# Second graph: own-neighbour mark by a VectorE maximum, shift diagonals by ScalarE instead of GpSimd

## The chip, the cores and the metric

One core of one Trainium2 chip runs the whole program, once per launch. The metric is the device time of that core in microseconds (us); less is better. A core has five engines that each work through their own queue of instructions in order: PE (TensorE, matrix products), DVE (VectorE, element-wise), ACT (ScalarE, functions of one input), POOL (GpSimd, element-wise) and SP (SyncE, which here issues most of the DMAs). They wait for each other by semaphores. "Before" and "after" mean the kernel without and with the change.

## The reference

3327 nodes with 256 features pass through two layers; each is a graph step and a feed-forward step, and each adds to the features `x`. The change lies in the graph step of the second layer, a graph attention:

```python
Wh = x @ W
e_src = Wh @ a[:d_out]
e_dst = Wh @ a[d_out:]
e = leaky_relu(e_src[:, None] + e_dst[None, :], 0.2)
mask = (adj > 0) | jnp.eye(N, dtype=bool)     # every node is its own neighbour
e = jnp.where(mask, e, NEG_INF)
alpha = softmax(e, axis=1)
h = alpha @ Wh
```

`adj` holds zeros and ones, and its diagonal is already one; the kernel pads it with zero rows and columns to 26 tiles of 128 (3328).

## The kernel before

The program runs the first graph, the mixture of experts, the second graph (`graph1`) and the attention heads one after the other. Helpers record every instruction, so that all carry one line (L61), and the profile is read by tile names. The `InOrder` helper of `graph1` keeps every engine's instructions in the order in which the Python code emits them.

`graph1` first joins, normalizes and projects the features (tiles `wh`, `dst`) and then goes through 7 blocks of target nodes (`blocks`: six of 4 tiles, the last of 2). Each block has 26 steps, one for every tile j of source nodes; `steps` is the list of all 182 pairs (b, j), and k counts them. In the loop at line 747, step k emits, in this order: the fixed loads of the next stage (from block 3 on, `heads_fixed`); a row load for the maximum (`load`); where j of step k+2 is a multiple of 4, the next `panel`; then `weights(k+2)`, `sign`, `masked(k+1)`, `gather(k)`, `finish`, `top`; and, at j = 16, 18 and 21, `shifts`, `rows` and `spread_rows` for the next block.

- `panel(b, g)` (line 669): SP loads four source tiles of the adjacency for each of the block's target tiles, one DMA of 256 KB per target tile, into one of three buffers `pan`. The group g = b holds the block's own diagonal squares (128x128). There each square is multiplied by `noti` (ones without the diagonal) and has the identity added, so that its diagonal is one: two POOL instructions for each target tile, 26 tiles in all, lines 677 and 678. Only `masked` of that panel, up to five steps later, needs the result.
- `weights(k)` (681): DVE forms `u` from the two broadcast rows `bc`, ACT takes the exponential.
- `masked(k)` (692): DVE forms `p` from the panel and `u`. `gather(k)` (703): PE multiplies `p` with `wh` into the accumulators `acc` (each product is two matmul records, eight records a step). `u` and `p` have four buffers each.
- `top` (515): in the first 16 steps of a block, DVE reduces eight rows of 1664 signs (tile `sg`) for the next block's maxima; `finish` (713) writes `x` in steps 1 to 4.
- `shifts(b)` (622): from these maxima DVE makes eight columns `ab` of shifts; `dg` is the identity scaled by each of them, two instructions of 128x512. DVE makes them for block 0, POOL for the others (line 639). `rows` multiplies `dg` by ones on PE, `spread_rows` copies the result into `bc` by ACT.
- POOL also makes `noti` once (line 419), issues the DMAs that store `x` (`xs`), and prepares tiles of the next stage (`igw`, `mask`).

Of the kernel before, what the change touches and what calls it, by code (L numbers as in the profile page):

```python
# [12 lines left out]
F32 = mybir.dt.float32  # L13
# [5 lines left out]
ALU = mybir.AluOpType  # L19
# [3 lines left out]
P = 128  # L23
# [78 lines left out]
class Net:  # L102
# [299 lines left out]
    def graph1_weights(self, pool):  # L402

        a = self.a

        self.gw = pool.tile([P, 2, D + 2], F32, name="gw")
        self.nc.scalar.dma_start(
            out=self.gw[:, :, :D], in_=a["gw"].rearrange("(k p) o -> p k o", p=P)
        )
        ga = pool.tile([P, 2 * D], F32, name="ga")  # L410
        self.nc.scalar.dma_start(out=ga, in_=a["ga"].partition_broadcast(P))
        self.vd = pool.tile([P, 2, P], F32, name="vd")
        self.shift = pool.tile([P, 1], F32, name="shift")
        self.noti = pool.tile([P, P], F32, name="noti")
        junk = pool.tile([P, D], F32, name="pj")

        def make(nc, ps):
            gw, shift = self.gw, self.shift
            nc.gpsimd.tensor_tensor(self.noti, self.ones, self.ident, ALU.subtract)
            for k in range(2):  # L420
                for i in range(2):
                    nc.vector.scalar_tensor_tensor(
                        junk, gw[:, k, :D], 1.0, ga[:, ts(i, D)], ALU.mult, ALU.mult,
                        accum_out=gw[:, k, D + i : D + i + 1],
                    )


            sq = junk[:, :2]
            nc.vector.tensor_tensor(sq, gw[:, :, D + 1], gw[:, :, D + 1], ALU.mult)
            nc.vector.tensor_copy(  # L430
                self.vd, gw[:, :, D + 1 : D + 2].to_broadcast([P, 2, P])
            )
            yield 1
            pv = ps()
            for k in range(2):
                nc.tensor.matmul(
                    pv[:, 0, :1], self.ones, sq[:, k : k + 1], start=(k == 0), stop=(k == 1)
                )
            nc.vector.tensor_scalar(shift, pv[:, 0, :1], 1e-30, None, ALU.max)
            nc.gpsimd.tensor_tensor(shift, shift, self.nhalf[:, :1], ALU.pow)  # L440
            nc.vector.reciprocal(shift, shift)
            nc.vector.tensor_scalar(shift, shift, 16.1, 1.0, ALU.mult, ALU.add)

        return make
# [37 lines left out]
    def graph1(self, xs, made, pool):  # L482
        tc, a, x = self.tc, self.a, self.x
        nc = InOrder(tc)
# [4 lines left out]
        with ExitStack() as ctx:  # L489
# [3 lines left out]
            ps = first.enter_context(tc.tile_pool(name="g1ps", bufs=2, space=PSUM))  # L493
            wk = first.enter_context(tc.tile_pool(name="g1w", bufs=4))
            s = self.small
            gw, shift, noti = self.gw, self.shift, self.noti

            W = D + 3
            wh = one.tile([P, NT, W], F32, name="wh")
# [122 lines left out]
            def shifts(b):  # L622


                tiles = blocks[b]
                n, t0 = len(tiles), tiles[0]
                es = e_src[:, t0 : t0 + n]
                m = s.tile([P, 4], F32, tag="m", name="m")[:, :n]
                ab = s.tile([P, 2, 4], F32, tag="ab", name="ab")[:, :, :n]
                for i, t in enumerate(tiles):  # L630
                    nc.vector.tensor_reduce(m[:, i : i + 1], tops.pop(t), AX.X, ALU.max)
                nc.vector.tensor_tensor(m, m, own[:, t0 : t0 + n], ALU.max)
                nc.vector.scalar_tensor_tensor(m, m, shift, es, ALU.subtract, ALU.add)
                nc.vector.scalar_tensor_tensor(m, m, 0.2, m, ALU.mult, ALU.max)
                nc.vector.tensor_tensor(ab[:, 0, :], es, m, ALU.subtract)
                nc.vector.scalar_tensor_tensor(ab[:, 1, :], es, 0.2, m, ALU.mult, ALU.subtract)
                dg = abp.tile([P, 2, 4, P], F32, tag="dg", name="dg1")
                for i in range(2):
                    (nc.gpsimd if b else nc.vector).tensor_tensor(
                        dg[:, i, :n, :],  # L640
                        self.ident.unsqueeze(1).to_broadcast([P, n, P]),
                        ab[:, i, :].unsqueeze(2).to_broadcast([P, n, P]),
                        ALU.mult,
                    )
                return dg

            def rows(b, dg):
# [21 lines left out]
            def panel(b, g):  # L669
                js = min(4, NT - 4 * g)  # L670
                pan = panp.tile([P, 4, 4, P], F32, tag="pan", name="pan1")
                for i, t in enumerate(blocks[b]):
                    nc.sync.dma_start(out=pan[:, i, :js, :], in_=a["adjt"][t][:, ds(4 * g, js), :])
                    if t // 4 == g:

                        d = pan[:, i, t % 4, :]
                        nc.gpsimd.tensor_tensor(d, d, noti, ALU.mult)
                        nc.gpsimd.tensor_tensor(d, d, self.ident, ALU.add)
                pans[b, g] = pan

            def weights(k):
# [49 lines left out]
            nc.vector.tensor_scalar(d2, e_dst, 0.2, None, ALU.mult)  # L731
            nc.vector.tensor_scalar(own, e_dst, shift, None, ALU.add)
            panel(*groups.pop(0))
            panel(*groups.pop(0))
            for k in range(8):
                if k in when:
                    load(*when[k])
            for t in blocks[0]:
                top(t, 2, PARTS[0])
            spread_rows(0, rows(0, shifts(0)))  # L740
            for k in range(3):
                if k in when:
# [4 lines left out]
            for k, (b, j) in enumerate(steps):  # L747

                if b > 2:
                    next(fixed, None)  # L750
                if k + 8 in when:
                    load(*when[k + 8])
                if k + 2 < len(steps):
                    if steps[k + 2][1] % 4 == 0 and groups:
                        panel(*groups.pop(0))
                    weights(k + 2)
                if k + 3 in when:
                    sign(*when[k + 3])
                if k + 1 < len(steps):
                    masked(k + 1)  # L760
                gather(k)
                if b and 1 <= j <= len(blocks[b - 1]):
                    finish(blocks[b - 1][j - 1])
                if k in when:
                    top(*when[k], PARTS[1])
                if b + 1 < len(blocks):
                    if j == 16:
                        dg = shifts(b + 1)
                    if j == 18:
                        pb = rows(b + 1, dg)  # L770
                    if j == 21:
                        spread_rows(b + 1, pb)
# [1244 lines left out]
```

## Time and profile before

| | |
|---|---|
| median of 5 runs | 2944.41 us (2933.12 to 2946.44) |
| the profiled execution | 2942.55 us, its span 2940.9 us |
| DVE, PE, ACT, POOL busy in the span | 2397.9, 2652.6, 1810.4, 972.1 us |
| second graph, blocks 0 to 6 | about 624 to 976 us of the span |
| POOL on `pan` (52 instructions of 128x128) | 447 to 2107 ns each, the two kinds' medians 898 and 782 ns |
| POOL on `dg` (12 instructions) | 1055 to 1489 ns each |

All times inside the profile count from the start of the span. A view by groups gives the count, the busy time and the mean of one shape; a view in order of time gives the start and the length of each instruction, and in square brackets how long its engine was idle before it and who ended that. Consecutive instructions of one engine overlap a little, so the distance from start to start is some hundredths of a microsecond below the length.

### The profile page before, as it was taken

What the parts mean: (1) busy time and instruction counts of PE and PEld (TensorE: products, weight loads), DVE (VectorE), ACT (ScalarE), POOL (GpSimd) and SP (SyncE); (2) the same over time, 40 slices, a digit from 0 to 9 for tenths busy, and PEclk for the clock granted to TensorE, in tenths of its full rate; (3) what the DMA queues carried; (4) which work ended last, traced back from release to release, by engine and by line L of the source; (5) the groups of instructions that cost most, each with busy time, mean ns of one, the idle gap of its engine ahead of it and who ended that gap; (6) DMA issues with size and microseconds to landing.
All of it is one profiled execution on the core that took longest, in us unless ns stands there. A gap on an engine that the chain in (4) does not pass through costs nothing. (4 is left out here: it accounts for less than half of the span.)

```text
span 2940.9 us, 125324 instructions
## 1 busy us (share of the span) xinstructions
PE 2652.6 (90%) x53422; PEld 1961.8 (67%) x53422; DVE 2397.9 (82%) x5619; ACT 1810.4 (62%) x5128; POOL 972.1 (33%) x1448
## 2 busy tenths in 40 slices
PE   7999998878989798999999999999989999999995
PEld 6878887757767666666666666666666666666664
DVE  5102643589999587889989999999999999999997
ACT  6420135555554477778777777777767677676674
POOL 6441634532141146544433333222122222122121
PEclk9999989989999799999999999999999999999998
DMA  9994568647775232333333433333433333433332
GB/s 376 358 324 141 182 208 268 211 177 265 270 245 178 74 91 75 109 100 114 116 102 110 121 116 111 112 116 111 123 113 110 116 115 115 119 114 109 116 110 78
DMA packets 258188, 449.70 MB, mean 153 GB/s; under 512 B 58816, under 2 KB 156608, under 8 KB 257504
## 3 DMA queue, kind: packets, MB, share of 16 engines
q1 hardware_dynamic: 245536, 417.50, 45.0%
q0 software_dynamic: 6576, 18.02, 1.7%
q8 instruction: 421, 6.90, 1.0%
q10 hardware_dynamic: 5520, 6.18, 0.7%
q14 instruction: 135, 1.11, 0.1%
HBM read 393.37 MB, written 25.88 MB: 143 GB/s over the span
## 5 line engine op out<-in xcount | busy, mean ns | idle before, releaser
L61 ACT ACTIVATE sc<-sc,anmax 128x512 f32<-128x512 f32 (+3 forms) x1568 | 1039.8, 668 | 109.0 <-DVE anmax L61 108.7
L61 PEld LDWEIGHTS po<-sc,vr 32*64 32x64 f32 x43728 | 660.8, 131 | 391.2 <-DVE sc L61 235.6
L61 PE MATMUL po<-sc,vr 32*64 32x128 f32 x43728 | 762.8, 275 | 114.0 <-DVE sc L61 75.1
L61 DVE STREAM_TRANSPOSE sc<-sc 128x2048 f32<-128x2048 f32 (+3 forms) x392 | 816.4, 2083 | 26.7 <-ACT sc L61 25.9
L61 PE MATMUL pqk<-kt,qt 64*128 64x512 f32 (+1 forms) x2944 | 738.8, 583 | 20.2 <-ACT qt L61 6.8
L61 DVE TENSOR_SCALAR_CACHE_REDUCE sc<-pqk 128x512 f32<-128x512 f32 (+2 forms) x1152 | 654.9, 623 | 49.8 <-PE pqk L61 48.4
L61 PEld LDWEIGHTS pqk<-kt,qt 64*128 64x128 f32 x2944 | 299.2, 186 | 232.2 <-issue 101.8
L61 PE MATMUL acc<-wh,p 128*128 128x259 f32 x1352 | 310.0, 387 | 34.8 <-DVE p L61 34.8
L61 PEld LDWEIGHTS acc<-wh,p 128*128 128x128 f32 x1352 | 254.1, 191 | 93.0 <-DVE p L61 52.5
L61 PE MATMUL acc<-y,pan 128*128 128x256 f32 x1352 | 304.1, 385 | 11.6 <-DMA pan<-in_adjt_dram 9.9
L61 ACT ACTIVATION_READ_ACCUMULATOR sc<-sc,anmax 128x1 f32 x1568 | 298.7, 191 | 0.0
L61 POOL TENSOR_TENSOR ot<-ot,sxd 128x512 f32<-128x512 f32 x83 | 105.7, 1274 | 579.1 <-ACT ot L61 566.1
L61 PEld LDWEIGHTS acc<-y,pan 128*128 128x128 f32 x1352 | 258.2, 193 | 52.6 <-issue 17.1
L61 DVE CUSTOM_DVE_ANT_0 sc<-pqk,mask 128x512 f32<-128x512 f32 (+3 forms) x416 | 242.3, 636 | 25.0 <-PE pqk L61 24.4
L61 ACT ACTIVATE u<-u,d 128x512 f32<-128x512 f32 (+1 forms) x182 | 125.2, 688 | 159.6 <-DVE u L61 159.3
L61 DVE SCALAR_TENSOR_TENSOR u<-bc,d 128x512 f32<-128x512 f32 (+1 forms) x182 | 136.0, 748 | 0.1
L61 DVE SCALAR_TENSOR_TENSOR p<-pan,u 128x512 f32<-128x512 f32 (+1 forms) x182 | 126.8, 696 | 10.3 <-PE acc L61 6.1
L61 ACT ACTIVATE junk<-ar 128x1664 bf16<-128x1664 f32 x52 | 82.7, 1591 | 65.8 <-DMA ar<-in_adj_dram 64.7
L61 ACT COPY qkv<-ptO 128x256 f32<-128x256 f32 x104 | 38.3, 368 | 134.7 <-PE ptO L61 134.4
L61 PE MATMUL ptO<-igw,ot 128*128 128x68 f32 x832 | 116.7, 283 | 3.7 <-issue 2.0
L61 PEld LDWEIGHTS ptO<-igw,ot 128*128 128x128 f32 x832 | 101.7, 192 | 22.5 <-issue 16.8
L61 DVE CUSTOM_DVE_ANT_0 sg<-sg,dst 128x1664 bf16<-128x1664 bf16 (+2 forms) x56 | 99.9, 1791 | 1.2 <-ACT dst L61 1.0
(340 smaller groups left out, 3020.7 us busy)
## 6 DMA issues: line engine op xcount, KB each, us to landing
vr<-vs SPq DMA_DIRECT2D x976, 128.0 KB
ar<-in_adj_dram SPq DMA_DIRECT2D x104, 832.0 KB
vr<-vs SPq DMA_DIRECT2D x544, 96.0 KB
pan<-in_adjt_dram SPq DMA_DIRECT2D x156, 256.0 KB
pan<-in_adjt_dram SPq DMA_DIRECT2D x26, 1024.0 KB
pan<-in_adjt_dram SPq DMA_DIRECT2D x20, 832.0 KB
w1e<-w SPq DMA_DIRECT2D x59, 256.0 KB
took<-places SPq DMA_DIRECT2D x59, 129.0 KB
```

The lines of the kernel that those rows point to most:

```text
L61: made = make(*args, **kw)
```

## The change

Three edits, all for `graph1`:

```diff
-        self.noti = pool.tile([P, P], F32, name="noti")
...
-            nc.gpsimd.tensor_tensor(self.noti, self.ones, self.ident, ALU.subtract)
...
                 for i in range(2):
-                    (nc.gpsimd if b else nc.vector).tensor_tensor(
-                        dg[:, i, :n, :],
-                        self.ident.unsqueeze(1).to_broadcast([P, n, P]),
-                        ab[:, i, :].unsqueeze(2).to_broadcast([P, n, P]),
-                        ALU.mult,
-                    )
+                    if b == 0:
+                        nc.vector.tensor_tensor(
+                            dg[:, i, :n, :],
+                            self.ident.unsqueeze(1).to_broadcast([P, n, P]),
+                            ab[:, i, :].unsqueeze(2).to_broadcast([P, n, P]),
+                            ALU.mult,
+                        )
+                        continue
+                    for j in range(n):
+                        nc.scalar.mul(dg[:, i, j, :], self.ident, ab[:, i, j : j + 1])
                 return dg
...
                         d = pan[:, i, t % 4, :]
-                        nc.gpsimd.tensor_tensor(d, d, noti, ALU.mult)
-                        nc.gpsimd.tensor_tensor(d, d, self.ident, ALU.add)
+                        nc.vector.tensor_tensor(d, d, self.ident, ALU.max)
                 pans[b, g] = pan
```

A diagonal square is now made by one DVE maximum with the identity, at the place in the order where the panel is loaded. The diagonals `dg` of blocks 1 to 6 are made by ACT, one instruction of 128x128 for each column of `ab`: eight a block, four in the last. The tile `noti` and its instruction are gone. No DMA is added, removed or moved.

More of the change, by code (lines that the diff above doesn't have):

```diff
@@ L495, in graph1 @@
             s = self.small
-            gw, shift, noti = self.gw, self.shift, self.noti
+            gw, shift = self.gw, self.shift
             W = D + 3
```

## The prediction

> **What bounds the kernel now.** I read the page, then busy time by stage, then the waits of the second graph, then the order of time around each edited place. All the edits lie in this stage. Its blocks run from about 624 to 976 us.
>
> The stage table (window; PE, PEld, DVE, ACT, POOL busy; granted clock, DMA share, GB/s):
>
> ```profile
> 665.00:719.00 54.00, 48.52 (x209) 38.94 (x210) 52.83 (x85) 30.38 (x36) 11.13 (x14) 1.00 0.73 253
> 719.00:775.00 56.00, 50.32 (x217) 39.81 (x215) 54.42 (x88) 30.71 (x36) 12.56 (x15) 1.00 0.73 256
> 775.00:829.00 54.00, 46.51 (x203) 37.66 (x203) 52.57 (x74) 29.88 (x35) 19.02 (x20) 1.00 0.81 266
> ```
>
> DVE is busy 97 to 98% of a block, PE some 90%; a DVE microsecond is a candidate for a microsecond of the whole. The waits of this stage say how far (us in total, times, longest):
>
> ```profile
> PE acc L61 <- DVE p L61: 34.8, 38, 3.2
> POOL pan L61 <- DMA pan<-in_adjt_dram: 34.2, 4, 13.3
> ...
> DVE p L61 <- PE acc L61: 6.1, 13, 0.9
> ```
>
> PE waits for DVE in steps with a row maximum. DVE waits for PE only 13 times, and those lie around a change of block: from j = 16 on there are no maxima, a DVE step is 1.27 us (u to u, 709.07 to 710.33 without its maximum) and PE's eight matmuls take some 1.76 (96 in 21.15 us). So PE sets the end from j = 16 until about j = 1 of the next block, and DVE from there to j = 16. The middle line is the one to remember: POOL, idle anyway, waits for the panel's DMA. The change puts an instruction with that wait into DVE's queue.
>
> **The maximum: its cost without waiting.** 26 DVE instructions of 128x128. The same operation at 128x512 takes 0.69 us, at 128x4 0.16; in proportion 128x128 takes 0.29, some 0.2 from start to start. 26 x 0.2 = 5.2 us in all, on DVE. Four of them (block 0) come after `own`, which starts at 615.13, when their panel (issued at 584.34) has long landed, and DVE works on without a gap to 620: +0.8.
>
> **The maximum: its wait.** It stands ahead of u(k+2); behind it in DVE's queue are u, p and the maxima, and ACT and PE wait for these. When the panel lands is read from POOL's first multiply, which waits for nothing else that is late; where DVE would want it, from the u at the same place. Blocks 1, 2 and 3, in order of time (start, length, engine, instruction, idle before it):
>
> ```profile
> 673.13 1.78 SPq L61 DMA_DIRECT2D pan<-in_adjt_dram  x4
> ...
> 674.29 0.74 DVE L61 SCALAR_TENSOR_TENSOR u<-bc,d 128x512 f32<-128x512 f32 x1
> ...
> 677.84 0.69 POOL L61 TENSOR_TENSOR pan<-pan,noti 128x128 f32<-128x128 f32 x1 [10.95 <-DMA pan<-in_adjt_dram]
> ```
>
> ```profile
> 738.51 0.75 DVE L61 SCALAR_TENSOR_TENSOR u<-bc,d 128x512 f32<-128x512 f32 x1
> ...
> 740.04 0.45 POOL L61 TENSOR_TENSOR pan<-pan,noti 128x128 f32<-128x128 f32 x1 [2.37 <-DMA pan<-in_adjt_dram]
> ```
>
> ```profile
> 800.41 4.91 SPq L61 DMA_DIRECT2D pan<-in_adjt_dram  x4
> ...
> 804.24 0.75 DVE L61 SCALAR_TENSOR_TENSOR u<-bc,d 128x512 f32<-128x512 f32 x1
> ...
> 805.64 3.76 PE L61 MATMUL acc<-wh,p 128*128 128x259 f32 x16 [1.00 <-DVE p L61]
> ...
> 809.87 0.45 POOL L61 TENSOR_TENSOR pan<-pan,noti 128x128 f32<-128x128 f32 x1 [7.78 <-DMA wk<-in_wk_dram]
> ```
>
> The page sees only the first tile's landing. The other three follow at between 0.45 us (the issue spacing, 1.78 / 4) and 1.03 us (262 KB at 255 GB/s); I take the middle, 0.73, so the last lands 2.2 us after the first (bounds 1.3 and 3.1), and DVE goes on 0.2 later.
> - Block 1: DVE held from 674.29 to 680.2, 5.9 us. PE then still has three steps, 5.3 us; p(25) comes at 681.5, p(28) at 685.3 against 681.3 before. +4.0.
> - Block 2: 738.51 to 742.4, +3.9. DVE's last wait for PE was at 735.50, so nothing takes it back; PE works off what it has until 746.4, which changes nothing for DVE.
> - Block 3: 804.24 to 812.3, +8.1. SP is late here with the next stage's loads; the profile puts POOL's wait down to one of these (`wk`, issued at 805.37, behind the panel), so the first tile may have landed a little before 809.87. PE has run dry (1.00 us idle already).
> - Block 4: landing 866.85 + 2.2 = 869.1 against 870.82: no wait, four maxima, +0.8.
> - Block 5: 928.64 + 2.2 against 929.43: 1.6 with the last maximum. Block 6: first at 967.51 against 967.70, some 0.7. PE is without a gap from 923.25 to the end of block 6, so these count nearly nothing: +0.2 for both after what POOL returns there.
>
> Sum of the waits on the path: 4.0 + 3.9 + 8.1 + 0.8 + 0.2 = 17.0.
>
> **What leaves POOL.** DVE and POOL slow each other:
>
> ```profile
> 718.92 0.74 DVE L61 SCALAR_TENSOR_TENSOR u<-bc,d 128x512 f32<-128x512 f32 x1
> 719.08 2.93 POOL L61 TENSOR_TENSOR dg<-ident,ab 128x512 f32<-128x512 f32 x2 [26.44 <-DVE ab L61]
> 719.59 1.52 DVE L61 SCALAR_TENSOR_TENSOR p<-pan,u 128x512 f32<-128x512 f32 x1
> ...
> 721.04 1.52 DVE L61 SCALAR_TENSOR_TENSOR u<-bc,d 128x512 f32<-128x512 f32 x1
> 721.17 1.14 PE L61 MATMUL acc<-wh,p 128*128 128x259 f32 x4 [1.26 <-DVE p L61]
> ```
>
> Alone, p takes 0.68 and u 0.74. During the `pan` instructions they take 0.94 and a maximum 2.08 to 2.14 instead of 1.88. Adding up what exceeds these lengths: block 1 from 679.5 on 0.6 (the 0.5 before that only shortened a wait for PE), block 2 0.9, block 3 1.7, block 4 1.9. Also POOL's `igw` copies, which stood behind block 3's squares and cost DVE 1.5 at 817 to 824, now run mostly while DVE is held: 1.2 back. Together -6.3.
>
> **The diagonals by ACT.** Eight instructions at j = 16, as soon as `ab` is there. The nearest rows are ACT copies and activations of 128x128 and 128x256 at 0.36 to 0.38 us, 0.27 to 0.4 from start to start; I take 0.30, eight take 2.4 us. `mul` of 128x128 with a scalar column is not in the trace: 0.27 is the lower bound, 0.40 (0.72 for 128x512 less 0.82 ns an element) the upper. Queued behind them is the exponential of u(k+3), ready at 719.6, now done at about 722.2; p(k+3) follows at 722.9, against 723.1 before. p(k+2) is there 0.85 earlier. PE therefore gains between 0.85 and -0.6 at each of the five changes of block that DVE leads into; I take -0.2 each, -1.0 in all. `rows` at j = 18 finds `dg` after 2.4 us instead of 2.9. At the sixth change PE sets the pace.
>
> **PE's clock.** After PE's 6.6 us idle ahead of 619.8 the granted clock is 0.50 in 619 to 630 and 1.00 again from 634. In block 3 PE would be idle for some 9 us (its work of 1.00 us before 805.64 to p at 813.6). At half the clock a step takes 3.5 us against DVE's 2.17; four p buffers and 0.3 to 0.4 us of spare a step up to j = 16 take that up nearly whole: +0.5, bounds 0 and 3.4.
>
> The Trainium skill, "TensorE: Matmul & The Clock Gate", Part 1, speaks against the change: it states that one idle window of about 3.4 us halves the clock, and one busy window of that length restores it. By that rule alone three held places with some 3.6, 3.6 and 9 us of PE idle would each lose an estimated 1.7 us of PE time, 5.1 in place of the 0.5 above, were nothing of it absorbed.
>
> **Sum** against the profiled execution: 0.8 + 17.0 - 6.3 - 1.0 + 0.5 = +11.0, so 2942.55 + 11.0 = 2953.6; `noti` (0.47 us of POOL at 388) was waited for by nobody. The 5 runs' median is 1.9 above the profiled execution: 2955.4, forecast **2955**.
>
> **The rivals.**
> - *Hidden*: the work in PE's hands covers blocks 1 and 2, since up to four p tiles lie ready there. For it: PE is busy until 690.8 and 746.4. Against it: after that DVE leads for twelve steps with no gap to give the time back. Then 11.0 - 3.4 - 3.0 = +4.6: 2949.
> - *Clock*: PE goes cold after each hold and, with DVE only 0.3 us a step behind it, stays the bound until j = 16: 3 x 3.4 in place of 0.5, +21: 2965. For it: 619 to 632, cold throughout 13 us. Against: PE was idle in part there.
> - *Relief* (faster): DVE's queue never waits, because the panels land before DVE gets there, as in block 4, and every slowed DVE instruction is its old self: 9.0 us for `dg` (six times 1.6, less in the last) and 8.4 for `pan`, less 26 x 0.2: -12.2: 2932. It decides once the holds of blocks 1 to 3 fall below some 5 us together; the trace has 17.9. Even then PE's rate around the changes of block keeps part of it.
>
> That the maxima wait somewhere else than said isn't open: order on DVE is that of the code.
>
> **How the numbers follow.** About 0.3% (8.8 us) can be told from no change. Forecast 0.60 (of it 0.09 ends within 8.8 us), clock 0.14, hidden 0.18 (0.15 within, 0.03 above), relief 0.08 (0.07 faster). Slower 0.51 + 0.14 + 0.03 = 0.68, same 0.25, faster 0.07. The unknown terms at their ends: last landing -2.7 to +2.7 over three blocks, ACT -3.3 to +4, clock to +3; so 2949 to 2965 for the forecast itself. To leave out no more than 2 in 10 the range goes down past the hidden case: 2945 to 2966.
>
> **What would show it.** Right: DVE idle 5 to 9 us ahead of `pan<-pan,ident` in blocks 1, 2, 3, by DMA, little in 4; p and u at 0.68 and 0.74 throughout; ACT `dg` near 0.36. Wrong: no DMA wait on DVE above 2 us, or ACT `dg` above 0.5, or a PE idle that ends in a wait of DVE for PE.

## The result and the profile after

| | before | after |
|---|---|---|
| median | 2945.02 us (50 runs) | 2951.15 us (30 runs) |
| ratio, 95% interval | | 1.0025 (1.0018 to 1.0032) |
| profiled execution: span | 2940.9 us | 2949.9 us |
| second graph: start of DVE's `own` to the end of the last gather | 361.7 us | 369.4 us |
| the rest of the span behind it | 1964.0 us | 1966.0 us |

Slower by a quarter of a per cent, 6 to 7 us; the stage with the edits accounts for 7.7. The rest, which nothing touches, lay between 1956.6 and 1970.3 us in the ten profiles of this study, so that its 2.0 us here mean nothing. The stage is steadier: counted from `own`, the same undisturbed step of two kernels agrees within some 0.1 us. So the experiments are read mostly by the stage.

The stage table of after, three long windows around the changes of block and four short ones inside the third (columns as before: PE, PEld, DVE, ACT, POOL busy; granted clock, DMA share, GB/s):

```profile
665.00:719.00 54.00, 46.67 (x199) 36.85 (x200) 48.05 (x76) 30.95 (x40) 2.33 (x4) 1.00 0.68 238
719.00:778.00 59.00, 52.53 (x219) 41.31 (x217) 53.32 (x92) 32.78 (x44) 2.16 (x4) 0.97 0.68 242
778.00:838.00 60.00, 49.59 (x208) 40.24 (x207) 51.24 (x88) 32.78 (x44) 7.96 (x14) 0.91 0.77 253
...
810.00:814.00 4.00, 0.00 (x0) 0.00 (x0) 0.00 (x0) 0.00 (x0) 2.71 (x8) 0.86 0.98 380
814.00:818.00 4.00, 0.00 (x0) 0.00 (x0) 2.06 (x6) 0.13 (x1) 0.00 (x0) 0.50 0.84 255
...
822.00:826.00 4.00, 4.00 (x17) 3.38 (x16) 4.00 (x7) 2.81 (x3) 0.00 (x0) 0.86 0.66 196
826.00:830.00 4.00, 4.00 (x20) 3.46 (x19) 4.00 (x5) 2.82 (x3) 0.00 (x0) 1.00 0.81 211
```

POOL has nearly left the stage, and DVE, the bound, is no longer busy 97% of it but 89, 90 and 85%. From 810 to 814 PE, DVE and ACT do nothing (POOL copies tiles of the next stage) while the DMA share is 0.98: they wait for a transfer. The waits of the stage (total us, times, longest):

```profile
DVE pan L61 <- DMA pan<-in_adjt_dram: 15.3, 14, 5.2
PEld pb L61 <- issue: 10.5, 12, 7.6
ACT bc L61 <- PE pb L61: 7.6, 1, 7.6
PE pb L61 <- issue: 7.5, 1, 7.5
DVE p L61 <- ACT u L61: 7.4, 8, 1.1
```

The first line is POOL's old line with DVE in POOL's place. The last is new too: 1.13 us at each of the first five changes of block, where ACT makes the diagonals. Whether that one costs anything is seen below. Block 1, in order of time:

```profile
677.04 0.29 DVE L61 TENSOR_TENSOR pan<-pan,ident 128x128 f32<-128x128 f32 x1 [2.98 <-DMA pan<-in_adjt_dram]
677.64 0.29 DVE L61 TENSOR_TENSOR pan<-pan,ident 128x128 f32<-128x128 f32 x1 [0.30 <-DMA pan<-in_adjt_dram]
678.30 0.29 DVE L61 TENSOR_TENSOR pan<-pan,ident 128x128 f32<-128x128 f32 x1 [0.37 <-DMA pan<-in_adjt_dram]
679.21 0.29 DVE L61 TENSOR_TENSOR pan<-pan,ident 128x128 f32<-128x128 f32 x1 [0.61 <-DMA pan<-in_adjt_dram]
679.41 0.75 DVE L61 SCALAR_TENSOR_TENSOR u<-bc,d 128x512 f32<-128x512 f32 x1
...
680.82 7.26 PE L61 MATMUL acc<-wh,p 128*128 128x259 f32 x32 [1.29 <-DVE p L61]
```

DVE is ready at 674.06 and reaches its u at 679.41. The tiles land 0.6 to 0.9 us apart, 2.2 us from first to last. PE's three steps in hand last until 679.5; then it idles 1.29. Block 2:

```profile
742.57 0.29 DVE L61 TENSOR_TENSOR pan<-pan,ident 128x128 f32<-128x128 f32 x1 [1.75 <-DMA pan<-in_adjt_dram]
...
745.23 0.74 DVE L61 SCALAR_TENSOR_TENSOR u<-bc,d 128x512 f32<-128x512 f32 x1
...
746.63 9.40 PE L61 MATMUL acc<-wh,p 128*128 128x259 f32 x32 [2.02 <-DVE p L61]
```

Block 3 is the worst:

```profile
814.69 0.29 DVE L61 TENSOR_TENSOR pan<-pan,ident 128x128 f32<-128x128 f32 x1 [5.16 <-DMA pan<-in_adjt_dram]
...
817.03 0.75 DVE L61 SCALAR_TENSOR_TENSOR u<-bc,d 128x512 f32<-128x512 f32 x1
...
818.43 13.73 PE L61 MATMUL acc<-wh,p 128*128 128x259 f32 x50 [8.84 <-DVE p L61]
```

And the change of block, with the diagonals on ACT:

```profile
663.95 2.45 ACT L61 ACTIVATE dg<-ident,ab 128x128 f32<-128x128 f32 x8 [0.92 <-DVE ab L61]
664.57 0.68 DVE L61 SCALAR_TENSOR_TENSOR p<-pan,u 128x512 f32<-128x512 f32 x1
...
665.30 2.01 PE L61 MATMUL acc<-wh,p 128*128 128x259 f32 x8 [0.42 <-DVE p L61]
666.30 1.32 ACT L61 ACTIVATE u<-u,d 128x512 f32<-128x512 f32 x2
...
667.04 0.69 DVE L61 SCALAR_TENSOR_TENSOR p<-pan,u 128x512 f32<-128x512 f32 x1 [1.13 <-ACT u L61]
667.16 1.88 PE L61 MATMUL pb<-dg,ones 128*128 128x512 f32 x4
...
668.87 10.65 PE L61 MATMUL acc<-wh,p 128*128 128x259 f32 x48
```

Before, at this place:

```profile
664.47 1.53 DVE L61 SCALAR_TENSOR_TENSOR p<-pan,u 128x512 f32<-128x512 f32 x1
...
666.05 2.01 PE L61 MATMUL acc<-wh,p 128*128 128x259 f32 x8 [1.27 <-DVE p L61]
```

There p took 1.53 us beside POOL and PE idled 1.27; now p takes 0.68 and PE idles 0.42. The next p is held 1.13 us by the late exponential and ends at 667.73, yet PE has no idle there: it makes the rows (`pb`) from 667.16 to 669.0 and asks for this p only then.

The sum can be followed step by step: how much later than before the same u starts, both counted from `own` (us).

| at | after - before | e1: diagonals only | e4: block 3's hold alone | e5: best |
|---|---|---|---|---|
| block 0, j = 16 | +0.75 | 0.00 | +0.74 | -0.06 |
| block 0, j = 22 | +0.33 | -0.42 | +0.32 | -0.48 |
| block 1, j = 16 | +3.72 | -1.10 | +0.74 | -1.02 |
| block 2, j = 3 | +2.88 | -1.95 | -0.10 | -1.87 |
| block 2, j = 16 | +6.31 | -1.70 | +0.61 | -2.13 |
| block 3, j = 3 | +5.47 | -2.55 | -0.23 | -2.98 |
| block 3, j = 8 | +13.44 | -2.56 | +8.18 | -2.58 |
| block 3, j = 16 | +10.59 | -2.78 | +5.34 | -3.33 |
| block 4, j = 3 | +9.63 | -3.05 | +4.37 | -4.30 |
| block 4, j = 16 | +8.53 | -3.06 | +3.28 | -6.21 |
| block 5, j = 3 | +7.69 | -3.91 | +2.43 | -6.45 |
| end of the last gather | +7.70 | -3.91 | +2.42 | -6.45 |

The column of after rises at a hold, falls in the same block as DVE, no longer slowed by POOL, makes up some of it, and falls by 0.84 at each of the next four changes of block. At the first change only 0.42 has reached DVE when block 1's hold begins; in e1, where nothing holds DVE there, the other 0.43 follows two steps into block 1.

### The profile page after: what moved, and what is told of

The parts are those of the page before. It is cut to its first block, busy times and chain, and to the rows that moved or that the text cites. A ratio compares the mean times of both kernels' runs of the same rounds, so it can differ in the third digit from the quotient of the medians.

```text
span 2949.9 us, 125284 instructions
## 1 busy us (share of the span) xinstructions
PE 2659.6 (90%) x53422; PEld 1964.4 (67%) x53422; DVE 2386.3 (81%) x5645; ACT 1820.6 (62%) x5172; POOL 907.8 (31%) x1383
## 5 line engine op out<-in xcount | busy, mean ns | idle before, releaser
L61 DVE SCALAR_TENSOR_TENSOR p<-pan,u 128x512 f32<-128x512 f32 (+1 forms) x182 | 117.8, 647 | 14.6 <-ACT u L61 7.4
L61 DVE SCALAR_TENSOR_TENSOR u<-bc,d 128x512 f32<-128x512 f32 (+1 forms) x182 | 128.5, 706 | 0.1
L61 POOL DMA_DIRECT2D xs<-x x26 | 14.2, 548 | 357.0 <-DVE x L61 334.4
```

The source lines that it names most:

```text
L61: made = make(*args, **kw)
```

## The experiments

e4, e7 and e8 were executed once each, so that only their profiles are read.

**e1, the diagonals alone.** The squares stay on POOL, `dg` is made by ACT.

```diff
-                        nc.vector.tensor_tensor(d, d, self.ident, ALU.max)
+                        nc.gpsimd.tensor_tensor(d, d, noti, ALU.mult)
+                        nc.gpsimd.tensor_tensor(d, d, self.ident, ALU.add)
```

> Only the diagonals of the shifts go to ScalarE; the squares stay on GpSimd (multiply and add). Theory (VectorE is held by the panel's DMA; ScalarE's diagonals are a gain, because the rows matmuls stand between the two gathers and cover the late exponential): from VectorE's own to the end of the last gather 3.8 us less than before (361.7 to 357.9), PE idle 0.42 us instead of 1.27 at each change of block. Rival (the eight ScalarE instructions delay the exponential and cost as much as they give): within 1 us of before.

Measured: stage 357.8 us, 3.9 below before; ratio 0.9991 (0.9981 to 1.0001), which alone would not tell it from nothing. At the first change:

```profile
661.22 2.45 ACT L61 ACTIVATE dg<-ident,ab 128x128 f32<-128x128 f32 x8 [0.92 <-DVE ab L61]
...
662.57 2.01 PE L61 MATMUL acc<-wh,p 128*128 128x259 f32 x8 [0.42 <-DVE p L61]
```

PE's idle is 0.42, as in after. This half of the change is a gain; the rival falls.

**e2, the maximum alone.** `dg` back on POOL.

```diff
-                    for j in range(n):
-                        nc.scalar.mul(dg[:, i, j, :], self.ident, ab[:, i, j : j + 1])
+                    (nc.gpsimd if b else nc.vector).tensor_tensor(dg[:, i, :n, :], ..., ALU.mult)
```

> Only the maximum goes to VectorE; the diagonals of the shifts stay on GpSimd. Theory: the change's loss without its gain, 369.4 + 3.8 = 373.2 us for the stage, 11.5 above before, about 2956 us; VectorE held 5, 4 and 7 us in blocks 1, 2, 3. Rival (the stage's loss comes from ScalarE, the holds are hidden by p tiles that PE still has): 362 to 364 us.

Measured: stage 376.5, ratio 1.0044 (1.0030 to 1.0059), median 2951.6 against 2940.0 in the same session. The holds are those of after; the rival falls. 3.3 us more than expected, 2.9 of them at the change from block 4 to 5:

```profile
897.07 2.62 POOL L61 TENSOR_TENSOR dg<-ident,ab 128x512 f32<-128x512 f32 x2 [27.34 <-DVE ab L61]
897.15 0.97 DVE L61 SCALAR_TENSOR_TENSOR ab<-wh,m 128x4 f32<-128x4 f32 x1 [0.23 <-issue]
...
900.29 3.53 PE L61 MATMUL acc<-wh,p 128*128 128x259 f32 x8 [2.47 <-DVE p L61]
903.62 2.09 PE L61 MATMUL pb<-dg,ones 128*128 128x512 f32 x4
...
907.56 0.69 DVE L61 SCALAR_TENSOR_TENSOR p<-pan,u 128x512 f32<-128x512 f32 x1 [1.61 <-PE acc L61]
```

These 2.9 have two parts. First, POOL's `dg` begins before DVE's second `ab` (in before 0.2 us after it), and this 128x4 instruction takes 0.97 us instead of 0.15; DVE is 1.2 us later, and PE's idle is 2.47 instead of 1.26. Then the gather takes 3.53 us instead of 2.01, since the granted clock is 0.50 from 900.6 to 904.0 (windows of this run): from this gather to the next PE takes 5.26 us instead of 3.57, 1.7 more, and DVE soon waits for PE 1.61 us. Half a clock costs here because it falls where PE sets the pace. Only one profile shows it at this place.

**e3, the maximum later.** Each square's maximum right ahead of the `masked` step that reads it (blocks 1 to 6).

```diff
                 p = ep.tile([P, 4, P], F32, tag="p", name="p")
+                if b > 0 and j // 4 == b and j % 4 < n:
+                    d = pans[b, b][:, j % 4, j % 4, :]
+                    nc.vector.tensor_tensor(d, d, self.ident, ALU.max)
```

> The change, but in blocks 1 to 6 each square's maximum stands right ahead of the masked step that reads it, instead of at the panel's load. Theory: no hold, as the panel has landed; 0.8 (block 0) + 0.2 - 0.1 - 2.1 - 1.1 (blocks 1 to 4: four maxima of 0.2 less what GpSimd's squares cost) - 3.8 (diagonals) = 6.1 us below before, 355.6 us for the stage, about 2939 us. Rival (VectorE pays for the maxima themselves, or the wait only moves to the masked step): 365 us or more.

Measured: stage 359.8, 2.0 below before; ratio 0.9992 (0.9982 to 1.0003). The holds are gone, but only a third of the expected gain came. Where the rest went:

```profile
689.35 0.29 DVE L61 TENSOR_TENSOR pan<-pan,ident 128x128 f32<-128x128 f32 x1
689.77 0.69 DVE L61 SCALAR_TENSOR_TENSOR p<-pan,u 128x512 f32<-128x512 f32 x1
...
691.64 0.28 DVE L61 TENSOR_TENSOR pan<-pan,ident 128x128 f32<-128x128 f32 x1
692.06 0.69 DVE L61 SCALAR_TENSOR_TENSOR p<-pan,u 128x512 f32<-128x512 f32 x1
```

0.42 us from the maximum to the p that reads it, against 0.20 from one maximum to the next u, which doesn't (679.21 to 679.41 in after). Four a block in blocks 1 to 4: 16 x 0.22 = 3.5 us of the 4.2 that are missing.

**e4, one hold of three.** As e3, for blocks 1 and 2 only (`b in (1, 2)`).

> The change with the late maximum in blocks 1 and 2 only, so that of the three long holds block 3's is left. Theory: stage 369.4 - 3.2 (block 1: 3.4 held net, against 0.2) - 3.5 (block 2) = 362.7 us; the step from before to after over block 3 stays 8.0 at the hold and 5.0 at j = 16. Rival (the holds add up through PE's halved clock): with PE warm from blocks 1 and 2, block 3 alone costs under 3 us at j = 16.

Measured: stage 364.2, 1.5 above the expectation (e3's price for eight squares, 8 x 0.22, is 1.8). Over block 3 the lag rises from -0.23 to +8.18 and is +5.34 at j = 16: 5.6 us, in after 5.1 (+5.47 to +10.59), and the rival had under 3. So block 3's loss does not need the holds before it, nor a clock that they lowered.

**e5, the maximum one step ahead.** In the loop, ahead of `weights(k + 2)`, the square that `masked(k + 1)` reads; block 0's four between its `rows` and `spread_rows`, where DVE waits 3.29 us for `pb`.

```diff
...
+                    mb, mj = steps[k + 1]
+                    if mj // 4 == mb and mj % 4 < len(blocks[mb]) and mb:
+                        d = pans[mb, mb][:, mj % 4, mj % 4, :]
+                        nc.vector.tensor_tensor(d, d, self.ident, ALU.max)
...
                     weights(k + 2)
```

> The change, but each square's maximum stands one step ahead of the masked step that reads it, with a u instruction between the two (so that VectorE doesn't read at once what it has just written), and block 0's four stand where VectorE waits for the first broadcast rows. Theory: against the run with the late maxima 0.75 us (block 0) and 16 x 0.22 us (blocks 1 to 4) less: 359.8 - 4.3 = 355.5 us for the stage, 6.2 below before, ratio 0.998. Rival (a maximum costs 0.42 us of VectorE wherever it stands): 359 us.

```profile
689.69 0.29 DVE L61 TENSOR_TENSOR pan<-pan,ident 128x128 f32<-128x128 f32 x1
689.89 0.75 DVE L61 SCALAR_TENSOR_TENSOR u<-bc,d 128x512 f32<-128x512 f32 x1
690.55 0.68 DVE L61 SCALAR_TENSOR_TENSOR p<-pan,u 128x512 f32<-128x512 f32 x1
```

Measured: 0.20 from the maximum to u, stage 355.3, ratio 0.9976 (0.9963 to 0.9989), median 2938.7 against 2944.2. The p that follows does not read that u and starts 0.09 us before its end (689.89 + 0.75 against 690.55), so the 0.42 of e3 lies in what p reads and not in p. e5 is faster than before, and its stage is 14.2 us shorter than that of after: the change was right in what it moved and wrong in where it put the maximum.

**e6, four panel buffers** (`bufs=4` for `g1pan`), the maximum at its place.

> The change with four panel buffers instead of three, the maximum at its place. Theory (the hold is the panel's DMA, which starts only when a buffer comes free some steps earlier): SyncE may start it four steps earlier, the holds go, 369.4 - 14.9 = 354.5 us. Rival (the DMA queue is full at the changes of block, so an earlier issue lands no earlier): holds of blocks 1 to 3 stay above half, 362 us or more.

Measured: stage 361.4, between the two and nearer the rival; ratio 0.9985 (0.9976 to 0.9995). In block 1 the panel has now landed, and in block 3 it still has not:

```profile
675.43 0.89 DVE L61 TENSOR_TENSOR pan<-pan,ident 128x128 f32<-128x128 f32 x4
676.23 0.74 DVE L61 SCALAR_TENSOR_TENSOR u<-bc,d 128x512 f32<-128x512 f32 x1
```

```profile
799.01 4.54 SPq L61 DMA_DIRECT2D pan<-in_adjt_dram  x4
...
807.43 0.29 DVE L61 TENSOR_TENSOR pan<-pan,ident 128x128 f32<-128x128 f32 x1 [2.88 <-DMA pan<-in_adjt_dram]
```

From the last u ahead of a hold to the first behind it the lag rises by 0.8, 2.7 and 6.4 us in blocks 1, 2, 3 (5.5, 4.5 and 8.0 in after). A buffer more cures block 1, where a buffer was what the DMA waited for: the issue moves from 1.2 us to 6.2 us ahead of DVE's arrival. In block 3 it moves only from 2.9 us to 5.5 us ahead, and the first tile lands 8.4 us after it (8.1 in after). There SP issues row loads and the next stage's loads until just ahead of the panel (`fgw` at 798.48, the panel at 799.01); that these set the landing is not shown, as no run takes them away.

**e7, the rows matmuls one step later** (`if j == 19` in place of 18).

> The change with the rows matmuls one step later (j = 19), so that they no longer stand on PE between the gathers of steps 18 and 19. Theory (they cover the exponential that ScalarE's diagonals delay): PE idles some 0.6 us more ahead of gather(19) at the five changes of block, stage 372 to 373 us. Rival (the gain is only that VectorE's two instructions are no longer slowed): 369.4 as in the change.

Measured: stage 373.0, 3.6 above after.

```profile
667.29 0.69 DVE L61 SCALAR_TENSOR_TENSOR p<-pan,u 128x512 f32<-128x512 f32 x1 [1.13 <-ACT u L61]
...
668.04 2.01 PE L61 MATMUL acc<-wh,p 128*128 128x259 f32 x8 [0.47 <-DVE p L61]
...
669.89 1.88 PE L61 MATMUL pb<-dg,ones 128*128 128x512 f32 x4
```

The same late p now holds PE, 0.47 us more at this change. At the four later changes the lag falls by some 0.12 instead of 0.84 (4.57 to 4.45 from block 1 to block 2). So the rows matmuls are the cover of the late exponential, and without them most of the gain of the diagonals is gone. The 0.47 is not all of the difference; the rest was not traced, and no run moves the rows while POOL makes `dg`.

**e8, no marks in blocks 0 to 5.**

> The change without the marks in blocks 0 to 5 (left out: the squares' diagonals there are what the adjacency holds). What the marks cost in all: theory 361.7 - 0.6 - 0.9 - 2.9 - 1.9 - 3.9 = 351.5 us for the stage, 17.9 below the change. Rival (a good part of the change's time is ScalarE's or the clock's): 356 us or more.

Measured: stage 352.3, 17.2 below after and 9.5 below before; the rival falls. The marks of blocks 0 to 5 cost 9.5 - 3.9 = 5.6 us on POOL (e1 less e8), 17.2 as the change has them, and 3.0 in e5.

## Why the prediction was right, and where its sizes were off

Forecast: slower, 2955 within 2945 to 2966, +11.0 over the profiled execution. Measured: 2951, the stage +7.7. Term by term, from the table of lags:

| term | forecast | measured |
|---|---|---|
| block 0's four maxima | +0.8 | +0.8 |
| block 1: hold less what POOL gave back | 4.0 - 0.6 = +3.4 | 0.33 to 3.72: +3.4 |
| block 2 | 3.9 - 0.9 = +3.0 | 2.88 to 6.31: +3.4 |
| block 3 | 8.1 - 1.7 - 1.2 = +5.2 | 5.47 to 10.46 (at p, j = 16): +5.0 |
| block 4: no wait | 0.8 - 1.9 = -1.1 | -1.1 |
| blocks 5 and 6 | +0.2 | 0.0 |
| diagonals on ACT | -1.0 | -0.42 - 4 x 0.84 = -3.8 |
| PE's clock | +0.5 | 0.0 |
| sum | +11.0 | +7.7 |

*The holds* were right in mechanism and size. The step that gave them, the place of POOL's first wait for the DMA against DVE's u at the same point of the order, put the first tile 3.6, 1.5 and 5.6 us behind DVE in blocks 1, 2, 3; measured were 3.0, 1.8 and 5.2. In block 3 that was in part luck: the issue came only 2.9 us ahead of DVE (before: 3.8), but the tile landed 8.1 us after it (before, POOL began 9.5 us after it). The guess of 2.2 us from the first to the last tile was 2.2, 2.5 and 2.1. DVE's idle time itself was 4.3, 3.3 and 6.4 us, less in blocks 1 and 2 than the 5 to 9 named as a sign of being right. In block 5 the lag rises by 2.3 us at j = 16 and is back at 7.7 in block 6: PE sets the pace there, and the wait costs nothing, as forecast.

*POOL's return* was right: no u or p of the stage takes more than 0.76 us any more except one p beside `igw` (0.88 at 806.64), and block 4, where nothing holds DVE, gives -1.1 as forecast.

*The diagonals* were the term that was mis-sized: "PE therefore gains between 0.85 and -0.6 [...] I take -0.2 each". The instruction was sized right: 0.39 us, 2.45 us for eight, forecast 2.4; and so was the late p, 0.41 us earlier than before where 0.2 was said. What was missed is PE's queue: after gather(18) come the rows matmuls, 1.9 us, so the p that is late is not asked for until they are done, and the 0.85 us of the p before it comes through whole. That is the upper end of the stated bounds; e1 shows the gain, e7 takes its cover away. This term makes 2.8 of the 3.3 us between forecast and measurement.

*The clock*: the forecast's mechanism is there and its price is not. In after the clock is halved after block 2's hold (0.51 in the window 748.0 to 751.4) and after block 3's (0.50 from 814 to 818, whole again by 826). Yet the lag falls in these blocks by about what POOL returns, and DVE waits for PE nowhere between 737.7 and 793.8, nor between 795.6 and 855.2. The Trainium skill ("TensorE: Matmul & The Clock Gate", Part 1) has the rule that an idle window of about 3.4 us halves the clock. The run agrees that the clock falls, for 3.4 us after block 2, but here PE's idle ahead of it was only 2.02 us at 746.6, and after block 1's 1.29 us it did not fall. The forecast had PE busy through block 2's hold in one place and idle for 3.6 us in another; neither came. The estimate of 1.7 us lost at each hold did not come either, because DVE led by more than PE lost; where PE sets the pace, in e2, it did.

*The rivals.* Hidden falls: PE's stock of p tiles covers PE, not DVE, and DVE leads from there on; blocks 1 and 2 kept 3.4 us each. Clock falls by the table and e4. Relief falls for the change as made. Its condition, maxima that wait for nothing, is what e5 builds, and there the stage gains 6.5 us of the 12.2 that the rival added up; the forecast had said that PE's rate would keep a part.

## What to carry to other kernels

An instruction moved from an idle engine to the bounding one takes its waits along: a wait that cost nothing there (34 us of POOL's) holds whatever stands behind it in the new queue (15 us of DVE's here), however short the instruction itself is. Put such an instruction as late as its reader allows, but with another instruction between the two. And to price a delay, follow it to the engine that needs the result: what stands in that engine's queue ahead of it decides whether it is paid.

## What was not expected of the hardware

- A DVE instruction that reads what the one just before it wrote starts 0.42 us after it (maximum of 128x128, then p), one that doesn't 0.20 us after (e3 against e5): 0.22 us for each such pair, more than the 0.20 of the maximum itself.
- PE's clock was halved after idle times of 2.02 us (after, 746.6) and 2.47 us (e2, 900.3), for about 3.4 us each; it was not halved after 1.78 us (before, 815.6). The first cost nothing, since DVE set the pace; the second fell where PE did, with 1.7 us lost.
- POOL copies of one input (`igw`) slow DVE as well: p 0.88 instead of 0.68, a row maximum 2.08 instead of 1.88 (after, 806.64 and 807.45). Even a 128x4 instruction of DVE took 0.97 instead of 0.15 beside POOL's `dg` (e2, 897.15).
